# One core: the load of x as a whole image, or in four strips

## The chip, the cores and the metric

The kernel runs on one core of a Trainium2 chip. The metric is the device time of one execution in microseconds, lower is better. Times that follow are from single runs and from one execution taken by the hardware profiler. In the trace five engines appear: PE (TensorE, matrix products; PEld is its loading of weights), DVE (VectorE), ACT (ScalarE), POOL (GpSimd) and SP (SyncE), which does no arithmetic here and issues nearly all DMAs. An instruction waits on semaphores for what it needs[...].

## The reference

The input x is (32, 56, 56, 96): 32 images of 56 by 56 points with 96 channels, float32. Two layers are computed for every image on its own:

```python
# layer 0: a mixture of 4 experts sets the weights of each image
pooled = jnp.mean(x, axis=(1, 2))
rw = sigmoid(pooled @ Wr + br)                      # (b, 4)
h = relu(bn(einsum('bhwc,bcm->bhwm', x, Wk) + ...)) # Wk = sum_e rw * Wpw, 96 -> 384
h = relu(bn(cond_dw(h, Wdw, bdw, rw)))              # 3x3 depthwise, 384 channels
x = bn(einsum('bhwm,bmf->bhwf', h, Wk2) + ...) + x  # Wk2 = sum_e rw * Wpwl, 384 -> 96
# layer 1 on the 3136 points of an image
t = x.reshape(b, 3136, 96)
t = t + attn(layernorm(t))  # 96 -> 192, relu, FFT over the points, a complex relu, inverse FFT, 192 -> 96
t = t + ffn(layernorm(t))   # 96 -> 384 -> 96, values rounded to 8-bit floats
```

What matters here: the mean over a whole image must be known before any weight of that image, and the FFT needs all points of an image before it can go on.

## The kernel before, in words

The images are worked on one after another, overlapped like a pipeline: while one image is in its convolution, the one before it is in its FFT and feed-forward part. An image lies on chip as 96 partitions (channels) by 3136 columns of float32, 1176 KB. There are two such places, `xpad` (line 333), used in turn: image b takes the place of image b - 2. `xs[b]` (line 334) is the part of the place that holds the image; a margin of zeros stands before and behind it.

The stages, as generators of the program:

- `loads` (line 597) copies x of image b from memory into its place by one DMA on SP's queue. Image 0 is loaded ahead of it (line 341).
- `mixing` (605) sums x over the image on VectorE (the tile `pooled`), finds the experts' weights `rw` with a small product `ps_rw` and a sigmoid, and makes the image's weights `wk` and `wk2` and the constants `small` from them.
- `expansion` (675) makes the 384 channels from x: products `ps_pw` on TensorE, emptied by ScalarE into `hp`.
- The depthwise convolution is split: `convolved_tensor` (710) does most of it on TensorE as products with small diagonal matrices (`ps_dw`), `convolved_vector` (754) the rest on VectorE, as a chain of eight multiply-adds (taps) on the tile `h` whose first tap and last relu are on ScalarE.
- `projection` (780) goes back to 96 channels (`ps_pwl`), and `projected` (802) adds the result into x in place, strip by strip, and stores each strip to memory (x<-x).
- `forward` (860), for two strips side by side, normalises a strip of x (products `ps_t_a`), multiplies by the 96 x 192 weights (`ps_w<-w1c,x`), does the first half of the FFT (`ps_a`), and stores the result g to memory (gd<-g). The strips are `FWD = [(0, 8), (8, 8), (16, 8), (24, 4)]` (line 64): first double column and number of double columns of 112 values. A strip is done in groups of four double columns, so that strips 0 to 2 have two groups and strip 3 has one. The products of a strip read the 8 values before it too. When the last `ps_w` of a strip is written out, the event "x read" of that strip is set (line 886).
- `frequency_loads` (927) gathers g of the whole image, in another order, into `g2` (g<-gd), in two pieces.
- `frequencies` (941), `nonlinearity` and `spectrum` do the other half of the FFT (`ps_b`), the complex relu, and the way back.
- `inverse` (1050) and `hidden` (1136) end the FFT (`ps_d`), do the feed-forward part (`ps_n`, `ps_f`) and store the output.

The order of all instructions is set when the program is built, by a planner (`Plan`, line 134). Each generator yields the engine that it needs next, and the events that it waits for; the planner keeps a clock for each engine and takes, again and again, the generator that can start first. At the same start the smaller priority number goes first: `loads` has 8, `mixing` 6, `convolved_vector` 5 (lines 1152 to 1156). An event of a DMA is set late by an estimate of its duration:

```python
    def arrives(nbytes, *key):
        plan.done(*key, late=1.4 + nbytes / 220e3)
```

So an edit to a generator can change the order of the work of the others, where it changes the times that the planner counts with. The real waits are put in by the compiler from what each instruction reads and writes; columns of a tile that don't overlap don't wait for each other.

In the trace nearly all instructions of VectorE, ScalarE, GpSimd and SP carry line 289, and those of TensorE line 585: the helpers that issue them. They are told apart by the names of their tiles.

Of the kernel before, what the change touches and what calls it, by code (L numbers as in the profile page):

```python
# [48 lines left out]
C = 96  # L49
# [3 lines left out]
N = S * S  # L53
# [6 lines left out]
PB = 2 * S  # L60
NS = 4
SW = S // NS
SQ = SW // 2
FWD = [(0, 8), (8, 8), (16, 8), (24, 4)]
# [47 lines left out]
PE, DVE, ACT, POOL, SP = "PE", "DVE", "ACT", "POOL", "SP"  # L112
# [180 lines left out]
def kernel(  # L293
# [30 lines left out]
    def psum(name):  # L324
        ps = psp.tile([128, 1024], F32, tag="ps", name=name)
        if plan is not None:
            for _ in range(min(40, int((plan.idle() - 0.3) / 0.19))):
                nc.tensor.matmul(ps[:PB, 0:PB], dftb_s, dftb_s, start=True, stop=True)
        return ps
# [4 lines left out]
    xs = [xpad[b % 2][:, S : S + N] for b in range(NB)]  # L334
# [25 lines left out]
    for c in range(2):  # L360
        for i in range(2):
            for odd in range(2):
                to, at = NQ * (2 * c + i) + odd, NQ * (2 * (c ^ odd) + i) + odd
# [9 lines left out]
    lo = VECS["rd"][0]  # L373
    in_vecs = vecs[:, lo : lo + 8].rearrange("p (n h) -> p n h", h=2)
    for kind in range(NKIND):
        at = 128 * kind
        while at < 128 * kind + 128:
# [3 lines left out]
            n = min(C - c, 128 - p)  # L381
# [13 lines left out]
    for r in range(2):  # L395
        at = SP64 * r + 8
# [12 lines left out]
    def turned(q):  # L409

        return (slice(32 * q, 128), slice(0, 128 - 32 * q)), (slice(0, 32 * q), slice(128 - 32 * q, 128))
# [113 lines left out]
    for r in range(2):  # L525
        at = slice(SP64 * r, SP64 * r + SP64)
# [41 lines left out]
    def as_halves(ap):  # L568
# [4 lines left out]
    V, W, A, P, Q = (  # L573
        Engine(plan, DVE, nc.vector), Engine(plan, DVE, nc.vector, True), Engine(plan, ACT, nc.scalar),
        Engine(plan, POOL, nc.gpsimd), Engine(plan, SP, nc.sync),
    )

    def mm(to, lhsT, rhs, start=True, stop=True, share=1):
        n, m = _size(to), _size(lhsT)
        if rhs.dtype == F32:  # L580
            us = 2 * max(0.00084 * n + 0.004, 0.00088 * m)
        else:
            us = 0.00042 * n + 0.004
        plan.tick(PE, us / share)
        nc.tensor.matmul(to, lhsT, rhs, start=start, stop=stop)  # L585
# [5 lines left out]
    def arrives(nbytes, *key):  # L591
        plan.done(*key, late=1.4 + nbytes / 220e3)
# [3 lines left out]

    def loads():
        for b in range(NB):

            yield SP, [(key, b - 2, s) for s in range(NS) for key in ("x read", "x1 by") if b >= 2]  # L600
            if b:
                Q.dma_start(xs[b], x[b])
            arrives(4 * C * N if b else 0, "x", b)

    def mixing():

        for b in range(NB):
            yield DVE, [("x", b)] + [("x1", b - 2, s) for s in range(NS) if b >= 2]
            pooled = mixp.tile([C, 1], F32, tag="pooled", name=f"pooled_{b}")
            V.tensor_reduce(pooled, xs[b], AX.X, ALU.add)  # L610
            pool_b = mixp.tile([C, 128], F32, tag="pool_b", name=f"pool_b_{b}")
            V.behind.tensor_scalar(pool_b, ones, pooled, 1.0 / N, ALU.mult, ALU.mult)
            rw = mixp.tile([128, NE + 1], F32, tag="rw", name=f"rw_{b}")
            yield POOL
            P.memset(rw[:, NE : NE + 1], 1.0)
            yield PE, (), 1
            ps = psum(f"ps_rw_{b}")
            mm(ps[:, 0:NE], pool_b, wr_s)
            yield DVE
            V.tensor_add(rw[:, 0:NE], ps[:, 0:NE], br_s)  # L620
            plan.release()
            yield ACT
            A.activation(rw[:, 0:NE], rw[:, 0:NE], AF.Sigmoid)
            yield DVE
            wk = mixp.tile([C, M], F32, tag="wk", name=f"wk_{b}")
            V.tensor_scalar_mul(wk, wpw_s[:, 0, :], rw[:C, 0:1])
            for e in range(1, NE):
                W.behind.scalar_tensor_tensor(wk, wpw_s[:, e, :], rw[:C, e : e + 1], wk, ALU.mult, ALU.add)
            yield DVE
            by = rw.rearrange("p (k e) -> p k e", k=1)  # L630
            prod = mixp.tile([128, NMIX, NE + 1], F32, tag="prod", name=f"prod_{b}", bufs=1)
            W.tensor_mul(prod, stk_s, by.to_broadcast([128, NMIX, NE + 1]))
            small = mixp.tile([128, NMIX], F32, tag="small", name=f"small_{b}")
            V.behind.tensor_reduce(small, prod, AX.X, ALU.add)
            mixed[b] = wk
            small_of[b] = small
            plan.done("wk", b)
            for c in range(NPE):
                plan.spawn("diagonals", 3, diagonals(b, c))
            yield DVE  # L640
            wk2 = mixp.tile([128, NC3, C], F32, tag="wk2", name=f"wk2_{b}")
            V.tensor_scalar_mul(wk2, wpwl_s[:, 0], rw[:, 0:1])
            for e in range(1, NE):
                W.behind.scalar_tensor_tensor(wk2, wpwl_s[:, e], rw[:, e : e + 1], wk2, ALU.mult, ALU.add)
            yield SP

            wk2s[b] = [wk2]
            for q in range(1, G):
                wk2q = mixp.tile([128, NPE, C], F32, tag=f"wk2_{q}", name=f"wk2_{b}_{q}")
                for to, at in turned(q):  # L650
                    Q.dma_start(wk2q[to], wk2[at, 0:NPE])
                wk2s[b].append(wk2q)
            arrives(4 * 3 * 128 * NPE * C, "wk2", b)

    def diagonals(b, c):
        yield POOL, [("dwt", b - 2, 1, 0)] * (b >= 2)
        taps = small_of[b][:, 9 * c : 9 * c + 9].rearrange("p (t k) -> p t k", k=1)
        P.tensor_mul(
            diag[b % 2][c],
            ident32.rearrange("p (k j) -> p k j", k=1).to_broadcast([128, 9, 32]),  # L660
            taps.to_broadcast([128, 9, 32]),
        )
        plan.done("diag", b, c)
# [486 lines left out]
    with tc.manual_schedule():  # L1150
        for name, priority, stream in (
            ("loads", 8, loads()), ("mixing", 6, mixing()), ("inverse", 1, inverse(0)),
            ("inverse", 0, inverse(1)), ("frequency loads", 0, frequency_loads()),
            ("frequencies", 1, frequencies()), ("forward", 0, forward(0)),
            ("forward", 0, forward(1)), ("projection", 7, projection()),
            ("vector", 5, convolved_vector()), ("tensor", 2, convolved_tensor()),
            ("expansion", 7, expansion()),
        ):
            plan.spawn(name, priority, stream)
        plan.run()  # L1160
# [114 lines left out]
```

## Time and profile before

| | us |
|---|---|
| median of 3 runs | 4425.33 |
| lowest and highest run | 4413.33, 4429.42 |
| the profiled execution | 4422.13 |
| its span, first to last instruction | 4420.3 |
| TensorE, sum of busy time | 4143.1 |
| VectorE | 3481.1 |
| ScalarE | 2596.1 |
| GpSimd | 1097.7 |

After the first three images the trace repeats itself with a period of about 133 us an image (from one load of x to the next 130.5 to 136.0).

How to read it: busy time is the sum of the durations of an engine's instructions. Matrix products are pipelined and their ends are modelled, so that a busy TensorE need not be at its peak. In a listing by time a line has the start, the duration (both in us), the engine, the line of the code, the operation, the tile written and the tiles read, and how many instructions were merged; in brackets the idle time before it, and what ended that time. "issue" means that the engine waited for nothing that the profile shows. A table of waits has the engine and tile that waited, what ended the waits, the total in us, how many times, and the longest.

### The profile page before, as it was taken

What the parts mean: (1) busy time and instruction counts of PE and PEld (TensorE: products, weight loads), DVE (VectorE), ACT (ScalarE), POOL (GpSimd) and SP (SyncE); (2) the same over time, 40 slices, a digit from 0 to 9 for tenths busy, and PEclk for the clock granted to TensorE, in tenths of its full rate; (3) what the DMA queues carried; (4) which work ended last, traced back from release to release, by engine and by line L of the source; (5) the groups of instructions that cost most, each with busy time, mean ns of one, the idle gap of its engine ahead of it and who ended that gap; (6) DMA issues with size and microseconds to landing.
All of it is one profiled execution on the core that took longest, in us unless ns stands there. A gap on an engine that the chain in (4) does not pass through costs nothing.

```text
span 4420.3 us, 119618 instructions
## 1 busy us (share of the span) xinstructions
PE 4143.1 (94%) x50924; PEld 2786.6 (63%) x50924; DVE 3481.1 (79%) x7224; ACT 2596.1 (59%) x4103; POOL 1097.7 (25%) x1015
## 2 busy tenths in 40 slices
PE   6989999999999999999999999999999999999999
PEld 4556666666666666666666666666666666665678
DVE  6778787878787888787787788787888788888763
ACT  2455666656565656566556666556666556666554
POOL 2012232222232221332222332222332222332222
PEclk9999999999999999999999999999999999999999
DMA  3343344433434433444433443433444433434431
GB/s 87 75 105 83 90 100 105 99 104 82 102 97 105 99 103 79 106 99 99 103 92 84 109 103 98 107 88 88 105 107 102 103 92 85 115 96 102 98 98 51
DMA packets 336040, 424.85 MB, mean 96 GB/s; under 512 B 134928, under 2 KB 254544, under 8 KB 332208
## 3 DMA queue, kind: packets, MB, share of 16 engines
q1 hardware_dynamic: 333172, 417.00, 37.6%
q8 instruction: 401, 6.57, 0.6%
q14 instruction: 131, 1.07, 0.1%
q10 hardware_dynamic: 2336, 0.20, 0.0%
HBM read 202.60 MB, written 205.06 MB: 92 GB/s over the span
## 4 chain that ended last, share of the span: by engine, by line
PE 55%; DVE 18%; ACT 12%; DMA 8%; issue 4%; POOL 2%; SPq 0%; ACTq 0%; POOLq 0%; DVEq 0%
PE ps_w L585 11%; PE ps_dw L585 8%; PE ps_pwl L585 8%; DVE h L289 8%; PE ps_pw L585 8%; PE ps_b L585 6%; DMA g<-gd 5%; PE ps_d L585 4%; ACT nt L289 3%; ACT h L289 3%; DVE z L289 3%; DVE ha L289 3%; DMA gd<-g 2%; PE ps_f L585 2%; POOL h L289 2%
## 5 line engine op out<-in xcount | busy, mean ns | idle before, releaser
L289 DVE SCALAR_TENSOR_TENSOR h<-hp,small,h 128x1792 f32<-128x1792 f32 (+2 forms) x768 | 1318.1, 1716 | 56.9 <-ACT h L289 43.6
L585 PE MATMUL ps_dw<-hp,diag 32*32 32x448 f32 x27648 | 884.1, 545 | 31.5 <-issue 26.2
L289 POOL CAST h<-h 128x784 fp8e5<-128x784 f16 x384 | 544.5, 1443 | 1389.1 <-DVE h L289 1387.5
L585 PEld LDWEIGHTS ps_dw<-hp,diag 32*32 32x32 f32 x27648 | 524.8, 103 | 330.9 <-issue 136.8
L585 PE MATMUL ps_pw<-x,wk 96*128 96x448 f32 (+1 forms) x1344 | 594.5, 567 | 12.5 <-ACT y L289 12.0
L289 ACT ACTIVATE hp<-ps_pw,small 128x896 f32<-128x896 f32 (+2 forms) x384 | 360.4, 947 | 385.9 <-PE ps_pw L585 385.5
L585 PE MATMUL ps_pwl<-h,wk 128*96 128x448 f32 x1344 | 528.0, 540 | 0.3 <-ACT hp L289 0.2
L585 PE MATMUL ps_b<-dftb_s,g 112*128 112x112 f32 x2816 | 372.0, 295 | 45.0 <-DMA g<-gd 37.5
L585 PEld LDWEIGHTS ps_w<-w_s,z 128*112 128x112 f32 (+1 forms) x2816 | 352.6, 178 | 88.1 <-ACT h L289 55.2
L585 PEld LDWEIGHTS ps_b<-dftb_s,g 112*128 112x128 f32 x2816 | 356.8, 209 | 81.5 <-ACT h L289 40.5
L585 PE MATMUL ps_w<-w_s,z 128*112 128x96 f32 (+2 forms) x2816 | 372.3, 286 | 33.0 <-ACT h L289 32.4
L585 PEld LDWEIGHTS ps_pwl<-h,wk 128*96 128x96 f32 x1344 | 213.8, 163 | 263.0 <-issue 262.2
L289 ACT ACTIVATE nt<-yt,nm,rstd_f 112x96 fp8e5<-112x96 f32 x896 | 331.3, 456 | 69.6 <-DVE nm L289 69.2
L585 PEld LDWEIGHTS ps_pw<-x,wk 96*128 96x128 f32 x1344 | 238.8, 191 | 200.8 <-issue 140.5
L585 PE MATMUL ps_w<-w1c,x 96*64 96x192 f32 x3584 | 340.3, 332 | 2.4 <-ACT g L289 1.4
L289 ACT ACTIVATE z<-ps_b,nl_s 128x448 f32<-128x448 f32 (+2 forms) x384 | 248.6, 692 | 159.8 <-PE ps_b L585 159.7
L289 ACT CAST h<-ps_f 128x784 f16<-128x784 f32 x384 | 292.7, 820 | 84.3 <-PE ps_f L585 81.8
L289 DVE SCALAR_TENSOR_TENSOR ha<-ps_w,rstd_a,nshift 128x192 f32<-128x192 f32 x896 | 309.7, 407 | 25.8 <-PE ps_w L585 21.5
L289 POOL TENSOR_TENSOR mir<-mir,z 128x448 f32<-128x448 f32 (+1 forms) x192 | 203.7, 1061 | 482.0 <-ACT mir L289 364.3
L289 POOL TENSOR_TENSOR x<-x,y 96x784 f32<-96x784 f32 x128 | 258.1, 2021 | 261.5 <-DVE y L289 261.5
L289 ACT ACTIVATE h<-ps_dw,small 128x448 f32<-128x448 f32 x384 | 223.5, 628 | 134.6 <-PE ps_dw L585 134.6
L289 DVE SCALAR_TENSOR_TENSOR x<-ps_pwl,small,x 96x896 f32<-96x896 f32 (+1 forms) x128 | 131.5, 1027 | 209.2 <-PE ps_pwl L585 209.2
(167 smaller groups left out, 5727.3 us busy)
## 6 DMA issues: line engine op xcount, KB each, us to landing
gd<-g SPq DMA_DIRECT2D x448, 192.0 KB
g<-gd SPq DMA_DIRECT2D x64, 672.0 KB
x<-in_x_dram SPq DMA_DIRECT2D x32, 1176.0 KB
x<-x SPq DMA_DIRECT2D x128, 294.0 KB
yt<-yd SPq DMA_DIRECT2D x128, 294.0 KB
out_dram<-x SPq DMA_DIRECT2D x128, 294.0 KB
g<-gd SPq DMA_DIRECT2D x64, 546.0 KB
x<-x SPq DMA_DIRECT2D x96, 336.0 KB
```

The source lines that it names most:

```text
L289: return getattr(self.namespace, name)(out, *args, **kw)
L585: nc.tensor.matmul(to, lhsT, rhs, start=start, stop=stop)
```

## The change

`loads` no longer copies an image by one DMA. It goes over the four strips of `FWD` and copies the columns of each by a DMA of its own: three of 896 columns and one of 448. Before the change it waited for the last reading ("x read") and the last store ("x1 by") of all four strips of the image before it in the place. Now each strip waits for those of its own strip and of the next one, since the next strip's products read 8 columns back. `mixing` waits for the four arrivals in place of one. The first image is loaded as before.

```diff
     def loads():
         for b in range(NB):
-
-            yield SP, [(key, b - 2, s) for s in range(NS) for key in ("x read", "x1 by") if b >= 2]
-            if b:
-                Q.dma_start(xs[b], x[b])
-            arrives(4 * C * N if b else 0, "x", b)
+            for s, (lo, n) in enumerate(FWD):
+
+                yield SP, [(key, b - 2, t) for t in (s, min(s + 1, NS - 1)) for key in ("x read", "x1 by") if b >= 2]
+                if b:
+                    at = slice(PB * lo, PB * (lo + n))
+                    Q.dma_start(xs[b][:, at], x[b, :, at])
+                arrives(4 * C * PB * n if b else 0, "x", b, s)
 
     def mixing():
 
         for b in range(NB):
-            yield DVE, [("x", b)] + [("x1", b - 2, s) for s in range(NS) if b >= 2]
+            yield DVE, [("x", b, s) for s in range(NS)] + [("x1", b - 2, s) for s in range(NS) if b >= 2]
             pooled = mixp.tile([C, 1], F32, tag="pooled", name=f"pooled_{b}")
             V.tensor_reduce(pooled, xs[b], AX.X, ALU.add)
```

## The prediction

> **What bounds the kernel now.** I read the page first: TensorE is busy for nearly the whole span, so time can only be won where it waits or runs slowly.
>
> ```profile
> span 4420.3 us, 119618 instructions
> PE 4143.1 (94%) x50924; PEld 2786.6 (63%) x50924; DVE 3481.1 (79%) x7224; ACT 2596.1 (59%) x4103; POOL 1097.7 (25%) x1015
> ```
>
> Then the table of waits, for TensorE's own waits that a DMA or the fetching of instructions ends:
>
> ```profile
> PE ps_b L585 <- DMA g<-gd: 37.5, 23, 3.1
> PE ps_dw L585 <- issue: 26.2, 27, 2.2
> ```
>
> (us in total, times, longest.) Both are to be placed in time. So I listed SyncE's queue and TensorE around one load of x. Times are start, duration:
>
> ```profile
> 1632.36 0.46 SPq L289 DMA_DIRECT2D x<-in_x_dram  x1
> 1636.43 1.08 SPq L289 DMA_DIRECT2D gd<-g  x2
> 1640.51 0.91 SPq L289 DMA_DIRECT2D g<-gd  x2
> ...
> 1635.43 9.50 PE L585 MATMUL ps_dw<-hp,diag 32*32 32x448 f32 x288
> 1648.17 1.77 PE L585 MATMUL ps_pw<-x,wk 96*128 96x448 f32 x4 [1.11 <-ACT y L289]
> 1651.64 7.21 PE L585 MATMUL ps_b<-dftb_s,g 112*128 112x112 f32 x48 [1.70 <-DMA g<-gd]
> 1658.85 4.73 PE L585 MATMUL ps_pwl<-h,wk 128*96 128x448 f32 x12
> ```
>
> The load of x goes out 4.07 us before the last two stores of g. These must land before the gather g<-gd may start, and TensorE then waits for the gather. The last images need no more x, which gives the same place without a load:
>
> ```profile
> 4161.57 1.09 SPq L289 DMA_DIRECT2D gd<-g  x2
> 4164.20 2.29 SPq L289 DMA_DIRECT2D g<-gd  x2
> ...
> 4160.56 9.51 PE L585 MATMUL ps_dw<-hp,diag 32*32 32x448 f32 x288
> 4173.31 1.77 PE L585 MATMUL ps_pw<-x,wk 96*128 96x448 f32 x4 [1.10 <-ACT y L289]
> 4174.91 5.51 PE L585 MATMUL ps_b<-dftb_s,g 112*128 112x112 f32 x48
> ```
>
> Without the load the gather is issued 2.63 us after the stores (4164.20 - 4161.57), with it 4.08 (1640.51 - 1636.43). ps_b then starts without a wait and takes 5.5 us, not 7.2. From dw's start to ps_pwl's start I get 23.42 us with the load and 19.70 without (ps_pwl at 4180.26); with the ps_rw that this image lacks (0.16), 19.86.
>
> I made the same listing for all 27 images from 428 us on whose load has a record. Means: gather issued 4.76 us after the stores (4.05 to 5.83); wait before ps_b 1.43; ps_b 6.56 (13 images at 7.0 to 8.7, mean 7.80; 14 at 5.41); dw to the next matmul 10.72 where 9.43 is the fastest; dw to ps_pwl 23.27. From one load to the next is always 109.1 to 110.5 us plus this stage (136.01 with 26.25, 130.68 with 20.88): **what the stage loses, the image loses**. Against 19.86 that is 3.4 us an image.
>
> The windows view (length, then busy time of PE, PEld, DVE, ACT, POOL, granted clock, DMA share, GB/s) says how full the DMA engines are with and without the load:
>
> ```profile
> 1634.00:1640.00 6.00, 5.75 (x166) 3.11 (x167) 6.00 (x7) 2.87 (x4) 5.37 (x4) 1.00 0.87 243
> 4158.00:4164.00 6.00, 5.28 (x125) 2.49 (x133) 6.00 (x9) 4.00 (x6) 4.33 (x4) 1.00 0.40 101
> ```
>
> Last, VectorE after the load, for the first reader of x:
>
> ```profile
> 1640.37 5.23 DVE L289 SCALAR_TENSOR_TENSOR h<-hp,small,h 128x1792 f32<-128x1792 f32 x2
> 1645.53 3.40 DVE L289 TENSOR_REDUCE pooled<-x 96x1 f32<-96x3136 f32 x1
> ```
>
> The reduction starts 13.2 us after the load's issue, behind a chain of convolution taps, and does not wait for x. The load's arrival is hidden; its traffic is not.
>
> [...]the page's instruction queue moved 6.57 MB in 401 packets, 16.4 kB each, and the "issue" gaps in dw fall at the load. [...]Here ps_b at 7.0 us or more follows waits (of ps_pw for y and of ps_b for g) that sum to 2.2 to 3.6 us, and 5.4 follows sums up to 1.54.
>
> **The change part by part.**
>
> *Where the strips go.* A strip waits for the x reads of its own and of the next strip of image b - 2. A read ends with the strip's last w1 product (ps_w<-w1c,x on TensorE). Those of strips 0 and 1 are through at 1701.4. The last two of an image end at 1627.2 and 1631.1; strip 2 needs two of them, one after the other, and strip 3 one, so strip 2's second is the one at 1631.1. Strips 1 and 2 both need strip 2, and strip 3 stands behind them in the generator: all three go where the whole load went. Only strip 0 leaves (96 x 896 x 4 = 344 kB of 1204), to about 1702, some 63 us ahead of the other three. 860 kB stay.
>
> *Issues on SyncE.* Three more a load, 93 in all, at 0.46 us: the three strips at the old place end 1.4 us after its start, the next issue comes 4.07 after it; 2.7 us of cover, cost 0. If it were gone, 0.9 us on the stores. Strip 0 comes behind the stores of 1700.94 to 1702.0; the next issue is at 1706.4. The wait it adds is over at 1701.4, so nothing queues behind it: cost 0.
>
> *Strip 0's transfer.* 344 kB at 243 GB/s is 1.4 us, from about 1703.3. The stores before it flow from 1702.0 to 1703.6; then the DMA engines are idle up to the next stores. Cost 0; bounds 0 and 1.4 us (a fetch of instructions behind it).
>
> *Smaller rows.* 3,584 and 1,792 bytes in place of 12,544. The stretch before (1630 to 1634), mostly stores of 3,072-byte rows, moved 231 GB/s: at worst 5% of 3.5 us, 0.2 us[...]. I take 0.
>
> *The reduction.* It now waits for four arrivals. By the planner's formula (line 592) x arrives 6.9 us after its issue, now some 4. But mixing has priority 6 and the chain of taps 5, at the same ready time, so it stays behind the chain: cost 0. Moved ahead it would push taps, ACT y and ps_pw by up to 3.4 us. Only for image 2 is VectorE idle there (5.78 us before 180.25), so the order of the first images may shift: -4 to +4 us once.
>
> *The relief.* The queue ahead of the last stores is 344 kB shorter: 1.4 us at 243 GB/s; bounds 0 (the remaining 860 kB still hold the stores) and 2.13 (4.76 - 2.63). I take 1.4: 860 kB at 243 GB/s are 3.5 us, gone about when the stores get to the engines. The gather then lands 1.4 us earlier. Per image, the smaller of the wait and 1.4 averages 1.03 us. Of the 13 slow ps_b, the sum of waits falls to 0.8 to 2.15, seven of them to 1.57 or less: I count those and half of the other six as 5.41, 10 x 2.39 / 27 = 0.9 us. The fetch gaps in dw (10.72 - 9.43 = 1.29) shrink too, but y's wait and the gather's stand behind them: 0. Sum 1.93 us an image, taken as 1.9 with the 0.1 at strip 0's place.
>
> 29 loads (b = 3 to 31) x 1.9 = 55 us. The profiled execution took 4422.1 (span 4420.3 and 1.8 around it): 4422 - 55 = 4367. The median of the runs is 3 higher: **4370**.
>
> **Rivals.**
> *No relief* (0.2): the 860 kB still arrive ahead of the stores[...]; the gather is held as now. For it: they are 71% of the load, in the same place. Against it: the queue would have to be longer than 3.5 us. Gain 0 to 0.7 us an image: 4405 to 4430, say 4420.
> *The stall moves with the strip* (0.13): strip 0's traffic holds an instruction block of TensorE before the dw of 1708.04, where there is no gap today. Price at most its transfer, 1.4 us x 29 = 41 us; with no relief 4466. It decides, over 0.5% slower, once it costs 0.76 us an image more than the relief gives. For it: fetch gaps of up to 3.9 us follow the whole load. Against it: 1.4 us of traffic, over about 3 us before dw.
> *Another order* (0.08): the shift in image 2 settles into another cycle of the planner; either sign, 4380 to 4460.
>
> **How the numbers follow.** The forecast gets 0.59, with its own range 4335 (2.95 us an image, the relief at 2.13) to 4398 (0.9). The measurement tells about 0.5%, 22 us, from no change. Faster: 0.59 and 0.06 of the rivals, 0.65. Same: most of "no relief", and small ends, 0.20. Slower: most of "the stall moves" and half of "another order", 0.15. The range takes in "no relief" and leaves out the two others' slow ends: 4335 to 4434.
>
> **What would show it.** Right: one load of x some 63 us ahead of the old place and three at it; the gather issued about 3.3 us after the last stores; the wait of ps_b for g under 15 us in total; ps_b near 5.4; a period near 131; the reduction still behind the taps. Wrong: the gather still 4.7 us behind the stores; new "issue" gaps at the dw 76 us past the load; or another order on VectorE in the middle images.

## The result, and the profile after

| | before | after |
|---|---|---|
| median of the runs on one chip, us | 4422.7 (4 runs, 4413.33 to 4429.42) | 4357.46 (4 runs, 4354.7 to 4361.77) |
| span of the profiled execution, us | 4420.3 | 4358.2 |
| mean granted clock of TensorE | 0.988 | 0.993 |

The ratio of the times is 0.9855, with a 95% interval of 0.9833 to 0.9876. The changed kernel is faster by about 65 us, and the time lies 13 us below the 4370 that were predicted.

The page of the kernel after, its span and busy times:

```profile
span 4358.2 us, 119852 instructions
PE 4110.8 (94%) x50948; PEld 2777.8 (64%) x50948; DVE 3476.5 (80%) x7224; ACT 2596.4 (60%) x4103; POOL 1100.6 (25%) x1015
```

TensorE's busy time is 32.3 us shorter (4143.1 - 4110.8) for the same products: part of the gain is products that run faster, and about half of it (62.1 - 32.3 us of span) is waits that are gone. The trace's record of the granted clock agrees: TensorE ran at half clock for 110.6 us in all before, and for 62.0 us after. The table of waits of the kernel after has the same two rows as before, and one that has grown (us in total, times, longest):

```profile
PE ps_pw L585 <- ACT y L289: 24.1, 23, 1.1
...
PE ps_b L585 <- DMA g<-gd: 16.1, 14, 2.2
...
PE ps_dw L585 <- issue: 7.4, 7, 2.0
```

The wait for the gather fell from 37.5 to 16.1 us, and the gaps by issue in dw, in which TensorE waits for nothing that the profile shows, fell from 26.2 to 7.4. The wait of `ps_pw` for ScalarE's y was 12.0 and is 24.1: it took back a part.

SyncE's queue and TensorE around the load of the kernel after that answers to the one shown of before (start, duration, then as before):

```profile
1539.23 0.53 SPq L289 DMA_DIRECT2D x<-in_x_dram  x1
...
1602.60 1.49 SPq L289 DMA_DIRECT2D x<-in_x_dram  x3
1606.73 1.09 SPq L289 DMA_DIRECT2D gd<-g  x2
1609.41 1.54 SPq L289 DMA_DIRECT2D g<-gd  x2
...
1605.73 9.49 PE L585 MATMUL ps_dw<-hp,diag 32*32 32x448 f32 x288
1618.48 1.77 PE L585 MATMUL ps_pw<-x,wk 96*128 96x448 f32 x4 [1.13 <-ACT y L289]
1621.21 5.58 PE L585 MATMUL ps_b<-dftb_s,g 112*128 112x112 f32 x48 [0.96 <-DMA g<-gd]
1626.78 4.73 PE L585 MATMUL ps_pwl<-h,wk 128*96 128x448 f32 x12
```

One strip goes out 63.4 us ahead of the other three, which go where the whole load went: 4.13 us ahead of the last stores of g. The gather follows the stores by 2.68 us and not by 4.08. The wait before `ps_b` is 0.96 us and not 1.70, and `ps_b` takes 5.58 us and not 7.21. From the start of dw (the products `ps_dw` of the listing) to that of `ps_pwl`, called the stage below, it is 21.05 us (1626.78 - 1605.73), where it was 23.42.

The same listing for 27 images of each kernel, from the second load of the steady part on, gives these means. `ps_b` is counted up to the start of the product behind it, some 0.17 us less than its line shows. The rest of an image is the time from one dw to the next less the stage.

| us an image | before | after | difference |
|---|---|---|---|
| gather's issue after dw's start | 5.80 | 4.19 | -1.61 |
| dw to the next product (9.4 without a gap) | 10.79 | 9.74 | -1.05 |
| wait for y | 0.37 | 0.81 | +0.44 |
| wait before ps_b | 1.40 | 0.56 | -0.84 |
| ps_b | 6.57 | 5.78 | -0.79 |
| of these, ps_b of 7 us and more, times | 13 | 4 | |
| stage, dw to ps_pwl | 23.29 | 21.00 | -2.29 |
| rest of the image | 109.80 | 109.93 | +0.13 |
| period | 133.11 | 130.97 | -2.14 |

Of the 62.1 us between the two spans, 3.1 are won ahead of the first stage of the steady part, 61.1 over the 28 periods from there to the last stage, and 2.2 are lost behind it.

The windows view of the kernel after, over six microseconds that begin 1.73 us before dw (columns as before):

```profile
1604.00:1610.00 6.00, 5.51 (x151) 2.90 (x164) 6.00 (x8) 3.17 (x5) 5.16 (x4) 1.00 0.77 214
```

The DMA engines are busy for 77% of it, at 214 GB/s; before it was 87% at 243. The load's traffic is less, and far from gone (40% without any load).

VectorE after the load of the kernel after, for the first reader of x:

```profile
1610.68 5.23 DVE L289 SCALAR_TENSOR_TENSOR h<-hp,small,h 128x1792 f32<-128x1792 f32 x2
1615.83 3.40 DVE L289 TENSOR_REDUCE pooled<-x 96x1 f32<-96x3136 f32 x1
```

The reduction stays behind the chain of taps, 13.2 us after the issue of the three strips (1615.83 - 1602.60), as before.

### The profile page after: what moved, and what is told of

The parts are those of the page before. It is cut to its first block, busy times and chain, and to the rows that moved or that the text cites. A ratio compares the mean times of both kernels' runs of the same rounds, so it can differ in the third digit from the quotient of the medians.

```text
span 4358.2 us, 119852 instructions
## 1 busy us (share of the span) xinstructions
PE 4110.8 (94%) x50948; PEld 2777.8 (64%) x50948; DVE 3476.5 (80%) x7224; ACT 2596.4 (60%) x4103; POOL 1100.6 (25%) x1015
## 3 DMA queue, kind: packets, MB, share of 16 engines
q8 instruction: 401, 6.57, 0.7%
q14 instruction: 133, 1.09, 0.1%
## 4 chain that ended last, share of the span: by engine, by line
PE 56%; DVE 19%; ACT 12%; DMA 6%; issue 4%; POOL 2%; SPq 0%; ACTq 0%; POOLq 0%; DVEq 0%
PE ps_w L585 11%; PE ps_dw L585 10%; PE ps_pwl L585 8%; PE ps_pw L585 8%; DVE h L289 8%; PE ps_b L585 5%; PE ps_d L585 4%; DMA g<-gd 4%; ACT nt L289 3%; ACT h L289 3%; DVE z L289 3%; DVE ha L289 3%; PE ps_f L585 3%; POOL h L289 2%; PE ps_a L585 2%
## 5 line engine op out<-in xcount | busy, mean ns | idle before, releaser
L585 PE MATMUL ps_dw<-hp,diag 32*32 32x448 f32 x27648 | 869.9, 544 | 12.3 <-issue 7.4
L585 PEld LDWEIGHTS ps_dw<-hp,diag 32*32 32x32 f32 x27648 | 533.7, 103 | 288.5 <-issue 94.0
L585 PE MATMUL ps_pw<-x,wk 96*128 96x448 f32 (+1 forms) x1344 | 595.1, 568 | 24.7 <-ACT y L289 24.1
L289 ACT ACTIVATE nt<-yt,nm,rstd_f 112x96 fp8e5<-112x96 f32 x896 | 331.4, 456 | 69.6 <-DVE nm L289 69.3
L585 PEld LDWEIGHTS ps_b<-dftb_s,g 112*128 112x128 f32 x2816 | 336.4, 199 | 56.5 <-ACT h L289 26.1
L585 PE MATMUL ps_b<-dftb_s,g 112*128 112x112 f32 x2816 | 351.2, 284 | 20.7 <-DMA g<-gd 16.1
L289 ACT ACTIVATE h<-h,small 128x1792 f32<-128x1792 f32 (+2 forms) x96 | 135.9, 1416 | 270.2 <-DVE h L289 270.1
```

What stands on the lines that cost most here:

```text
L289: return getattr(self.namespace, name)(out, *args, **kw)
```

## The experiments

The theory: the load stands ahead of the last stores of g on the same queue; with a quarter of it gone, the stores land earlier, the gather too, and so `ps_b` waits less. Call it A, as the expectations do. The theories against it: the form of the load does it (four DMAs and shorter rows; theory B of the expectations); the waits belong to the stage and not to the load; the gain is that of another order of instructions; or the early strip does something itself. The kernel before took 4432 to 4434 us (medians) beside these runs, not 4422.7, so that each is read by its ratio to the kernel before on the same chip, with its 95% interval. The changed kernel was not run again beside them, so that ratios 0.1 or 0.2% from its 0.9855 tell no difference from it.

### The form of the load without its place

The changed kernel, but each strip waits for all four strips, so that the four DMAs go together at the old place:

```diff
-                yield SP, [(key, b - 2, t) for t in (s, min(s + 1, NS - 1)) for key in ("x read", "x1 by") if b >= 2]
+                yield SP, [(key, b - 2, t) for t in range(NS) for key in ("x read", "x1 by") if b >= 2]
```

> The load in the same four strips, but all four still wait for all of the image before, so that all 1204 kB go out at the old place. Theory A (the bytes queued ahead of the last stores of g decide): as before, 4405 to 4428 us, gather issued 4.3 us or more after the stores. Theory B[...]: as with the change, 4347 to 4370 us, gather 3.2 us after the stores.

Measured: 4422.27 us against 4432.5, a ratio of 0.9978 (0.9968 to 0.9988). The stage is 23.30 us (23.29 before), the gather comes 5.42 us after dw (5.80 before). These are theory A's numbers (the gather is issued 4.42 us after the stores). The form of the load, with the other order of the first images that comes with it, is worth 0.2%, one seventh of the change's 1.45%; the rest needs strip 0 to be elsewhere.

### No load at all

The kernel before with only image 1 loaded; the images after it start from what their place holds. The time is read for what the load costs in all:

```diff
-            if b:
+            if b == 1:
                 Q.dma_start(xs[b], x[b])
```

> The kernel before without its loads of x from image 2 on (each image then starts from what the place holds, so the output is of other data). Theory A: the stage from dw to ps_pwl goes to 19.9 us in every image, 3.4 us x 29 less than before: 4325 us (4315 to 4335), gather 2.6 us after the stores, no wait for it. Theory C (the gather itself bounds the stage once the stores land): 4345 us or more, waits for the gather stay.

Measured: 4354.82 us, 0.9827 (0.9800 to 0.9855). All that the load costs is about 1.7%, not the 2.2% or more that the 3.4 us an image in the prediction stand for (3.4 x 29 = 99 us): the change has nearly all there is to have. The stage is 20.96 us, against 21.00 of the change. From the table of waits of the kernel without loads:

```profile
PE ps_b L585 <- DMA g<-gd: 9.1, 8, 2.0
```

Eight waits for the gather are left with no load in the way: theory C's time and waits, not A's. The stage of 19.86 that I had taken for "without a load" was that of a single image; it is the best of a scatter that reaches over 25 us in the changed kernel.

### The old traffic at the old place, with the new loads kept

The changed kernel, and behind its strip 3 a copy of strip 0 (344 kB) into a tile that nobody reads. The order of TensorE, VectorE, ScalarE and GpSimd is that of the changed kernel:

```diff
+    again = const([C, 8 * PB], F32, "again")
...
+                if b >= 2 and s == 3:
+                    Q.dma_start(again, x[b, :, 0 : 8 * PB])
```

> The changed kernel, which at the old place also copies strip 0 a second time, into a tile that nothing reads: strip 0 is early, but again 1204 kB go out ahead of the last stores of g. Theory A (the bytes there decide): the gain goes, ratio to the kernel before 0.995 to 1.003, gather 5.3 to 5.8 us after dw's start. Theory F (that strip 0 comes early is the gain): the ratio of the change, 0.983 to 0.988, gather 4.2 us after dw's start.

Measured: 4410.76 us against 4433.53, 0.9953 (0.9932 to 0.9974). Of the change's 1.45% about 1.0% is gone. Around one load, SyncE's queue:

```profile
1618.62 1.47 SPq L289 DMA_DIRECT2D x<-in_x_dram  x3
1620.14 0.42 SPq L289 DMA_DIRECT2D again<-in_x_dram  x1
1622.18 1.09 SPq L289 DMA_DIRECT2D gd<-g  x2
1626.30 0.91 SPq L289 DMA_DIRECT2D g<-gd  x2
```

The gather follows the stores by 4.12 us again (1626.30 - 1622.18; before 4.08, after 2.68). The waits, from this kernel's table:

```profile
PE ps_b L585 <- DMA g<-gd: 33.7, 21, 2.9
```

33.7 us, against 16.1 of the change and 37.5 before. The stage is 23.42 us, as before. One DMA of 344 kB, with nothing else changed, brings the wait back: this shows A. The profiled execution (span 4418.5) was the slowest of seven; by the medians a third of the gain stays. 0.2% may be the form of the load; what makes the remainder of it is not settled.

### How much may stay at the old place

The changed kernel with the load in two parts, the first early, the second at the old place. The cut is at 15, 8 or 4 double columns of 28:

```diff
-            for s, (lo, n) in enumerate(FWD):
+            for s, (lo, n, read) in enumerate([(0, 8, (0, 1)), (8, 20, (1, 2, 3))]):
-                yield SP, [(key, b - 2, t) for t in (s, min(s + 1, NS - 1)) for key in ("x read", "x1 by") if b >= 2]
+                yield SP, [(key, b - 2, t) for t in read for key in ("x read", "x1 by") if b >= 2]
```

The cut at 15:

> The load in two parts: 15 double columns (645 kB) where strips 0 and 1 have been read, 13 (559 kB) at the old place. Theory A: of the 1.2 us an image that the change leaves over the place without a load, about half goes: 4340 us (4330 to 4350), gather 2.8 us after the stores. Theory C: as with the change, 4352 to 4365 us. Theory D (traffic at the new place now holds TensorE's instructions there): gaps by issue in the dw that follows it, 4365 us or more.

The cut at 8, which is the change's own with one DMA and rows of 8,960 bytes in place of three:

> Strip 0 early, and the other 860 kB at the old place in one copy with rows of 8,960 bytes. Theory A: as with the change, ratio 0.983 to 0.988. If the short rows have a part of their own beyond what the split in place showed (0.2%): 0.989 to 0.993.

The cut at 4:

> The load in two parts: 4 double columns (172 kB) where strips 0 and 1 have been read, 24 (1032 kB) at the old place. Theory A with relief in proportion: half of the change's gain, ratio 0.990 to 0.995, gather 4.6 to 5.0 us after dw's start. If the relief has a threshold between 860 and 1032 kB: as with the split in place, 0.996 or more, gather 5.2 us or more. If any part that leaves is enough: 0.983 to 0.988.

Measured, with the others, by what stays at the old place (means of 26 or 27 images, us):

| bytes at the old place | kernel | gather after dw | ps_b of 7 us and more | stage | ratio |
|---|---|---|---|---|---|
| 0 | no load | 4.02 | 3 | 20.96 | 0.9827 (0.9800 to 0.9855) |
| 559 kB | cut at 15 | 4.00 | 4 | 21.08 | 0.9865 (0.9839 to 0.9890) |
| 860 kB | the change | 4.19 | 4 | 21.00 | 0.9855 (0.9833 to 0.9876) |
| 860 kB | cut at 8, one DMA | 4.54 | 7 | 21.59 | 0.9842 (0.9822 to 0.9863) |
| 1032 kB | cut at 4 | 5.21 | 17 | 23.23 | 1.0030 (1.0014 to 1.0047) |
| 1204 kB | strip 0 again | 5.30 | 17 | 23.42 | 0.9953 (0.9932 to 0.9974) |
| 1204 kB | four strips at the old place | 5.42 | 15 | 23.30 | 0.9978 (0.9968 to 0.9988) |
| 1204 kB | before | 5.80 | 13 | 23.29 | 1 |

The cut at 15 gives what theory C said, no more than the change, and none of its seven gaps by issue lies at the new place, so that D did not come true for 645 kB. The cut at 8 is A's number, and short rows are not needed. The cut at 4 is that of a threshold, not of relief in proportion: between 860 and 1032 kB the stage rises by 1.6 to 2.2 us. Below it less traffic brought no more (20.96 us with none, 21.00 with the change's 860 kB), and above it the stage won nothing (23.23 to 23.42 us, 23.29 before), though the gather is up to 0.6 us earlier than before.

The packet records of the traces show what moves the gather. The stores have rows of 3,072 bytes and the loads have others, so that the two can be told apart. Means over the same images, in us after dw's start:

| bytes at the old place | kernel | last packet of the load ends | first packet of the stores starts | last one ends |
|---|---|---|---|---|
| 0 | no load | | 2.11 | 4.07 |
| 559 kB | cut at 15 | 1.52 | 2.11 | 4.19 |
| 860 kB | the change | 2.53 | 2.13 | 4.29 |
| 860 kB | cut at 8, one DMA | 2.86 | 2.12 | 4.51 |
| 1032 kB | cut at 4 | 3.72 | 2.39 | 5.17 |
| 1204 kB | strip 0 again | 4.01 | 2.78 | 5.28 |
| 1204 kB | four strips at the old place | 3.94 | 2.66 | 5.37 |
| 1204 kB | before | 4.22 | 2.86 | 5.73 |

The gather goes out within 0.2 us of the end of the stores' last packet. With 860 kB the load is gone 0.4 to 0.7 us after the stores' first packets; with more, these start later (2.39 to 2.86 us, not 2.11 to 2.13), and it is still there for 1.2 us and longer. The gather's time rises steadily with the load's end; the step is in the stage, and in the slow `ps_b`: 3 to 7 up to 860 kB, 13 to 17 from 1032 kB on, each with at least 3.41 us at half clock (last section).

These runs also settle what the order of the instructions is worth. The kernel with four strips at the old place and the cut at 15 have the same order on TensorE, VectorE, ScalarE and GpSimd, and differ by 1.1% (0.9978 and 0.9865). The cut at 8 has the order of the kernel before, but for image 2's reduction and its small product one place earlier, and gains what the change gains.

The cut at 4 ends slower than before although its period, 133.13 us, is the same. Against before it is about 30 us late already after its first five images, whose order is another one, and 30 us still at the end of the loads (dw at 4190.72 against 4160.56): a loss that comes once. Where a strip is loaded changes the times that the planner counts with, and this kernel is sensitive to them.

### The whole load after the gather

The kernel before, with the load made to wait for the first piece of the gather:

```diff
-            yield SP, [(key, b - 2, s) for s in range(NS) for key in ("x read", "x1 by") if b >= 2]
+            yield SP, [(key, b - 2, s) for s in range(NS) for key in ("x read", "x1 by") if b >= 2] + [("g2", 2 * b - 4)] * (b >= 2)
```

> The whole load in one piece, but only after the first half of the image's second transform has read the gathered g, some 27 us past the old place; the planner then orders mixing anew. Theory A: the stage at the old place takes 19.9 us, as without a load; with an order as good as before 4325 us. Theory E (the later mixing, or the load beside the second gather and the loads of the inverse part, costs as much as is won): 4357 us or more.

Measured: 4840.36 us, 1.0917 (1.0890 to 1.0945). The planner puts the whole program in another order, an image takes 147 us in the mean (110 to 170 from load to load). From its table of waits:

```profile
POOL x L289 <- DVE y L289: 702.7, 128, 18.1
...
ACT h L289 <- PE ps_dw L585: 502.5, 78, 14.5
```

Of the traffic this says nothing. It says what a different order can cost here: 9%, six times what the change wins. About half of that is the clock, by an estimate: TensorE ran at half clock for 509.6 us, against 110.6 before, and half of the difference is 200 us.

### The gather in two parts

The rival "the stall moves with the strip" did not come true for strip 0. To see whether it can at all, and whether the rest of the gather's wait can be had, I let the columns of strips 0 and 1 of the gather's first piece (four DMAs of 192 KB) go as soon as they are stored, some 73 us after the load, and only the other 12 of 28 at the old place. On the changed kernel:

```diff
+    def gather(b, c, q0, q1):
+        k0, nk = GROUPS[0]
+        rows = gds[b][c, 2 * k0 : 2 * (k0 + nk), q0:q1].rearrange("(k i) q m -> i q k m", i=2)
+        for half in range(2):
+            at = S * c + NQ * half + q0
+            nc.sync.dma_start(g2[at : at + q1 - q0, 0:nk, :], rows[half])
...
+        early.add(b)
+        for c in range(2):
+            gather(b, c, 0, 16)
...
+                    if i == 0:
+                        plan.tick(SP, 0.36)
+                        gather(b, c, 16, NQ)
+                        continue
```

> The changed kernel, with the first gather of each image made in two steps: the columns of strips 0 and 1 as soon as they and the place are there, those of strips 2 and 3 where the whole gather stood, 12 of 28 columns; the order of every engine but SyncE is kept. Theory A (what the change leaves, 1.1 us an image, is still mostly the wait for the gather and the slow ps_b after it): stage 20.2 to 20.6 us, 0.5 to 0.8 us x 29 less than with the change, ratio to the kernel before 0.979 to 0.983. Theory G (what is left is the fetching of instructions, and the wait only takes its place): stage 20.9 us or more, ratio 0.984 to 0.988.

Measured: 4410.96 us against 4432.31, 0.9955 (0.9941 to 0.9970): slower than the change by about 1%, which neither theory had. At the old place it does what A says: `ps_b` starts without a wait at 1630.31 in the image whose dw starts at 1615.95, and the mean stage is 20.19 us. But the rest of an image is 112.48 us, not 109.93. SyncE and TensorE where the early part of the gather goes:

```profile
1683.41 1.08 SPq L289 DMA_DIRECT2D gd<-g  x2
1686.13 1.79 SPq L935 DMA_DIRECT2D g<-gd  x4
...
1685.07 7.49 PE L585 MATMUL ps_dw<-hp,diag 32*32 32x448 f32 x239
1696.32 3.52 PE L585 MATMUL ps_dw<-hp,diag 32*32 32x448 f32 x49 [3.76 <-issue]
```

In the middle of this dw TensorE stands still for 3.76 us and waits for nothing that the profile shows. In the changed kernel the same dw (1676.05, 8.79 us) has no gap. The windows view over six microseconds of this dw, first of the gather in two, then of the change:

```profile
1690.00:1696.00 6.00, 2.56 (x80) 1.45 (x69) 5.28 (x7) 0.76 (x1) 0.29 (x1) 1.00 0.99 120
```

```profile
1680.00:1686.00 6.00, 6.00 (x168) 3.85 (x157) 5.71 (x8) 2.36 (x4) 0.91 (x1) 1.00 0.02 5
```

The DMA engines are 99% busy in the one and 2% in the other. The gap is not all: the 49 products behind it take 3.52 us, and the same view shows why, by the granted clock of 0.52:

```profile
1696.32:1699.84 3.52, 3.52 (x50) 1.10 (x50) 0.00 (x0) 1.04 (x2) 0.00 (x0) 0.52 0.02 5
```

In all images of the gather in two:

```profile
PE ps_dw L585 <- issue: 69.3, 32, 4.5
```

69.3 us in 32 gaps, where the change has 7.4 in 7. The packet records tie the gaps to the packets of a queue of the kind that the page calls "instruction" (q8). It moves one packet of 16,384 bytes about every 11 us (401 in the 4358.2 us of the change); each of the 32 gaps ends 1.3 to 1.9 us after such a packet has ended (the gap shown ends at 1696.32, its packet at 1694.83), and so does each of the change's 7 (1.2 to 1.8 us) and of the 27 before (1.2 to 1.6 us). That the full DMA engines hold such a packet up was not shown: the records do not say since when a packet was due, and the 27 packets before last 1.09 us in the median, where all 401 last 1.07.

The same edit on the kernel before:

> The kernel before, its load whole and at the old place, with the same gather in two steps. It takes the late gather away[...]. Theory A with two channels (of the 2.15 us an image of the change 1.6 came by the gather and 0.6 by the fetching in dw): ratio 0.988 to 0.991. Gather alone: the ratio of the change or better, 0.980 to 0.987, gaps by issue in dw as before but hidden. Fetching alone: 0.995 or more.

Measured: 4451.12 us, 1.0049 (1.0034 to 1.0063). The stage falls by 2.31 us an image (23.29 to 20.98) and the rest rises by 2.46 (109.80 to 112.26). It is the same cost at the later dw, whatever the load does. In the stage the theory "gather alone" holds; the ratio is outside its range because none of the three counted the later dw. (The profiled execution, 4434.67 us, was the fastest of six; by its stages alone the kernel would be 4 us slower than before, and not 19.) So the two bills are separate: one for traffic ahead of the stores, one for traffic during the other dw. No kernel that was tried beats the change by more than the intervals tell.

## Why the prediction was right

*What leaves and what stays.* Right: strip 0 goes 63.4 us ahead (some 63 predicted), the three others go where the whole load went, and 860 kB stay.

*The relief.* Right, and shown by the copy of strip 0: the gather's issue after the stores fell from 4.76 to 3.21 us in the mean over the images, 1.55 where 1.4 was predicted. The reason given, that 860 kB are gone about when the stores get to the engines, is seen in the packet records: 2.53 us after dw's start, where the first of the stores start at 2.13.

*The wait and ps_b.* -0.84 and -0.79 us an image, against -1.03 and -0.9: the mechanism was right, the two terms together were too large by 0.3 us. Nine of the 13 slow `ps_b` went, ten were counted. The rule that they were counted by, waits that sum to 2.2 us or more, is only roughly right: before the change one was slow at 1.62 (the `ps_b` of 717.62), after it one at 1.92 (2936.19), and two at 2.1 were fast (1621.21 and 1753.25). What the record of the clock shows of this stands in the last section.

*The gaps in dw.* This is the step that failed. They were put at 0 with the argument that y's wait and the gather's stand behind them. They shrank by 1.05 us, and y's wait took back only 0.44. The prediction cut the relief at the wait of before, as if dw's end stood fixed. But the gap and the gather's wait shrink together, so that `ps_b` starts 1.45 us earlier after dw's start (10.79 + 0.37 + 1.40 against 9.74 + 0.81 + 0.56), not 1.03. The net 0.61 us make up for the 0.3 above; that two errors of opposite sign nearly cancel is luck. The "fetch gaps of up to 3.9 us" of the rival were read too large as well: the longest gap in this dw is 2.2 us, and in the dw of 1102.51, which is 3.9 us longer than the fastest, the gap is 1.95 us, and the granted clock is halved for 3.41 us from 1110.03 on.

*The sum.* 1.9 us an image was predicted, the traces show 2.14; in all 55 us were predicted, and the spans differ by 62. The 13 us that the median lies below the forecast are these 7 (the profiled execution after took 4360.07 us, 4367 was predicted), and 6 in how the two profiled executions stand to their medians: the forecast added 3 us, and the median after lies 2.6 below.

*What there was to win.* "Against 19.86 that is 3.4 us an image" was wrong: without loads the mean stage is 20.96, so that the load cost 2.3. The lower end of the range (4335) rested on the same image, by the relief of 2.13 (4.76 - 2.63). One image stood for a mean of 27.

*Strip 0's place, SP's issues, the reduction.* All at 0, and the rest of the image rose by 0.13 us in all (0.1 was taken). The reduction is where it was.

*The order of image 2.* As foreseen, the order changes there and nowhere else, apart from SyncE's new loads. VectorE before the change (start, duration, idle time before in brackets):

```profile
180.25 1.15 DVE L289 SCALAR_TENSOR_TENSOR x<-ps_pwl,small,x 96x896 f32<-96x896 f32 x1 [5.78 <-PE ps_pwl L585]
181.32 3.40 DVE L289 TENSOR_REDUCE pooled<-x 96x1 f32<-96x3136 f32 x1
```

and after it:

```profile
177.98 3.42 DVE L289 TENSOR_REDUCE pooled<-x 96x1 f32<-96x3136 f32 x1 [3.31 <-DMA x<-in_x_dram]
```

The reduction goes 3.34 us earlier, into time in which VectorE was idle. The first load of the steady part starts at 425.04 us and not at 428.39: 3.4 us won once, within the -4 to +4.

*The rivals.* "No relief" falls with the gather's times. "The stall moves with the strip" falls for 344 kB, since the later dw keeps its 8.79 us and no later dw has a gap by issue; with the 768 KB of the gather in two the later dw does get such gaps (3.76 us in the one shown). "Another order" falls too: the orders are the same after image 2, and the cut at 8 gains as much with the order of before. That the cut at 4 and the load after the gather did fall into other orders shows that the chance was not empty.

## What to carry to other kernels

A load whose arrival is hidden can still cost its traffic, if something small that is waited for is queued behind it: here 2.3 us an image. Take away only as much as lets the queue drain before that comes; more brought nothing here (a stage of 21.08 us with 559 kB at the old place, 21.00 with 860 kB). The place that it is moved to has to be looked at in the same way, with what runs there and the gaps by issue counted in (69.3 us in the gather in two). Before pricing what can be won at most, take the case without the cost over many images, not one.

## What the runs showed of the hardware

- The stage does not follow the gather's time in a straight line. From 4.0 to 4.2 us after dw it is 21.0 to 21.1, at 4.54 it is 21.59, and from 5.2 to 5.8 it is 23.2 to 23.4. `ps_b` takes 5.4 us or 7 and more, and nearly nothing between. The traces show that the two differ in the granted clock of TensorE, 0.51 and 1.00 below. The windows view over the middle of the slow `ps_b` of 1651.64, and over the fast one of 3383.26, both of the kernel before (columns as above):

```profile
1652.71:1656.07 3.36, 3.36 (x19) 3.36 (x17) 0.16 (x1) 1.68 (x3) 0.37 (x1) 0.51 0.99 292
3383.26:3388.67 5.41, 5.41 (x48) 5.41 (x49) 1.59 (x4) 4.42 (x8) 3.49 (x3) 1.00 0.70 208
```

- In the ten kernels other than the load after the gather, each of the 84 slow `ps_b` overlaps at least 3.41 us at half clock, and none of the 202 fast ones overlaps any. The record of the clock knows two values, 1 and 0.5, and nearly all its stretches at half clock last 3.41 us or a whole multiple of it; within a kernel they all begin on one grid of 3.413 us (the 21 before and the 11 after to within 0.01 us), which the waits do not move. So beyond their own length the waits mostly cost nothing, or 1.6 us, or 2.6 to 3.2 (lines of `ps_b` of 5.58 us, 7.21, and 8.16 to 8.80, before and after), and much the same sum of waits was slow in one image and fast in another (1.92 us ahead of 2936.19, 2.1 ahead of 1621.21). The half clock came after waits that were each under 3.41 us (0.79 and 1.12 us ahead of 2936.19). How much idle time it takes, and whether the grid is the clock's or that of its record, was not shown: no run set the idle time by itself.
- Without any load the gather is still late in seven images of 27 (4.4 to 5.3 us after dw, 3.7 to 3.9 in the others), and six of the dw have a gap by issue, of 0.92 to 3.58 us. In all seven a 16,384-byte packet of the instruction queue starts 2.0 to 2.2 us after dw, just as the stores' first packets do, and then the last store packets come one by one, 0.12 us apart. In none of the other 20 does such a packet start between 1.0 and 3.2 us. That the one holds up the other was not shown: the records do not name the DMA engine of a packet.
- A gap by issue of up to 4.5 us in TensorE's products, beside a gather that kept the DMA engines 99% busy at 120 GB/s (over the six microseconds from 1690.00), was more than I had expected of 768 KB. The half clock often follows: of the 17 stretches of it between 420 and 4200 us in the gather in two, 15 begin within such a gap or less than 2 us behind one. Together they cost 2.5 us an image.
